# Attention in two halves over two steps, in a fused state-space and attention kernel

## The chip, the core and the metric

The kernel runs on one core of a Trainium2 chip. The core has four compute engines that work side by side, each through its own list of instructions in order: TensorE (PE, matrix products and transposes, with a separate track PEld for loading weights), VectorE (DVE), ScalarE (ACT) and GpSimd (POOL). SyncE (SP) issues the transfers (DMA). Operands lie in SBUF; matrix products land in PSUM. The metric is the time of one whole execution on the device, in microseconds (us), lower is better.

## The reference

The input x is 16 images of 128 channels and 64 x 64 positions, so 16 sequences of 4096 tokens of 128 numbers. A first layer adds a selective state-space block; a second adds an attention with one fixed query per head and then a mixture of 64 experts. Cut to what the change touches:

```python
# layer 0, after GroupNorm: a recurrence over the tokens, d = 256 channels, n = 16 states
xc    = silu(causal_conv4(xs) + conv_b)
dt, Bm, Cm = split(xc @ W_xproj)
delta = softplus(dt @ W_dt + b_dt)
h_t   = exp(delta_t * A) * h_{t-1} + (delta_t * xc_t) * B_t      # per channel and state
y_t   = sum_n h_t * C_t
out   = (y + xc * D_param) * silu(z) @ W_out                      # added to x, transposed in height and width

# layer 1, after LayerNorm: 8 heads, a running softmax over all tokens up to t
k, v  = silu(x @ W_kv)                       # per head 128 numbers each
s     = q_proj . k
m_A   = cummax(s)
u_A   = cumsum(exp(s - m_A))
w_A   = cumsum(exp(s - m_A) * v)
output = mean over heads of w_A / u_A        # added to x
# then: LayerNorm, top-8 tokens for each of 64 experts, two-layer experts, scattered back
```

## The kernel before

The sequences are cut into blocks of 512 tokens: 8 blocks each, 128 in all. A main loop makes one *step* per block k. A step has 16 *slots*, one for each state n. In it four blocks are in work: block k in the recurrence; block k + 1 in the convolution, x-projection and delta; block k - 1 in its output projection; and block m = k - 9 in the attention. A wrapper keeps each engine's instructions in the order of the text; before the change the transfers, issued through `nc.sync`, are not under it.

The recurrence, with one scan per state and half of the channels:

```python
dap = tile_pool("dap", bufs=8); hp_ = tile_pool("hp", bufs=2); bcp = tile_pool("bcp", bufs=4)   # abridged
ps  = tile_pool("ps", bufs=3, space=PSUM); acc = tile_pool("acc", bufs=1, space=PSUM)           # abridged

def load_bc(k, n):        # B and C of one state, spread to 128 rows
    t = w["bc", n] = bcp.tile([P, 2, L], F32, tag="bc", name="bct")
    nc.sync.dma_start(t, w["bcs"][n : n + N + 1 : N, :].partition_broadcast(P))

def decay(k, n):
    for a in range(NH2):
        ACT.activation(da[:, a, :], w["delta"][:, a, :], AF.Exp, scale=a_neg[:, a, n : n + 1])

def scan(k, n):
    bx = bps.tile([P, NH2, L], F32, tag="bx", name="bx")                    # PSUM
    DVE.tensor_tensor(bx, w["du"], bc(bt[:, 0:1, :], [P, NH2, L]), ALU.mult)   # the product with B
    for a in range(NH2):
        DVE.tensor_tensor_scan(h[:, a, :], da[:, a, :], bx[:, a, :], <0.0 or state>, ALU.mult, ALU.add)
    POOL.tensor_tensor(da, h, bc(bt[:, 1:2, :], [P, NH2, L]), ALU.mult)     # the product with C

def keep_state(k, n):     # the last column, for the next block
    ACT.copy(gn[w["b"]]["state"][:, n, :], h[:, :, L - 1])

def add_y(k, n):          # eight transposes that add up in PSUM
    ...
```

The attention of a block of 512 tokens, in four chunks c of 128. A weight from token t' to token t is exp((s - m) at t' minus log u at t), computed as a product of two small matrices plus a mask:

```python
lh = wp.tile([P, L], F32, name="lh")            # 5 rows in each half in use
rh = wp.tile([P, L // P, 4, P], F32, name="rh")

def score_max(m):   # VectorE: running maximum, then s - max -> le; four transfers le -> lh
def score_exp(m):   # ScalarE: e = exp(le)
def score_sum(m):
    DVE.tensor_tensor_scan(s["mx"], bc(ones[:, 0:1], [P, L]), s["e"], ..., ALU.mult, ALU.add)
    ...             # TensorE: e transposed; ScalarE: to e1
def score_log(m):   # ScalarE: log; eight transfers mx -> rh; ScalarE: e = exp(-log)

def weights(m, c):
    for u in range(2):
        rows = slice(64 * u, 64 * u + 5)
        PE.matmul(rp, identb, bc(maskb.unsqueeze(1), [P, 4, P]), start=True, stop=False)
        PE.matmul(rp, lh[rows, bass.ts(c, P)], rh[rows, c].rearrange("p x t -> p (x t)"), start=False, stop=True)
        ACT.activation(wm[:, u].rearrange("p q g t -> p (q g t)"), rp, AF.Exp)

def attend(m, c):         # eight products weights x values -> ao_ps, eight narrow ones -> carry_ps
def carry_on(m, c):       # VectorE: carry += carry_ps
def attend_before(m, c):  # TensorE: what earlier chunks carry to this one
def finish(m):            # VectorE: xt += ao_ps / 8; transfer to t2_d
```

One step, cut to the parts that move:

```python
def slot(n):
    if n == 0:  attend(mp_, 3); attend_before(mp_, 2); add_y(prev, 14); key(m, 0..2); carry_on(mp_, 2)
    if n == 1:  attend_before(mp_, 3); add_y(prev, 15); key(m, 3..4); carry_on(mp_, 3); finish(mp_); score(m, 0); ...
    if n == 3:  load_exp(); score(m, 1); score_max(m); gate(prev)
    if n == 4:  out_proj(prev); score_exp(m); conv(nxt, 0)
    if n == 5:  residual(prev); score_sum(m); conv(nxt, 1)
    if n == 6:  score_log(m)
    if n == 7:  conv_silu(nxt); gate_silu(cur); xproj(nxt)
    if 7 <= n <= 9: value(m, ...)
    if n == 9:  delta(nxt)
    if n == 10: load_exp(); ln_center(mn)      # and its square on ScalarE
    if n == 11: ln_scale(mn)
    if 11 <= n <= 14: weights(m, n - 11)
    if n >= 12: attend(m, 0), (m, 1), (m, 2) in slots 12, 13, 14; carry_on(m, 0) in 13, carry_on(m, 1) in 15
    if n == 13: ln_apply(mn)

for n in range(N):
    scan(cur, n); load_bc(n + 4); keep_state(cur, n - 1)
    if n == N - 1: delta_x(nxt)
    slot(n)
    add_y(cur, n - 2)
    if 3 <= n <= 6 or n >= 10: decays(k, n, 2)     # up to five states ahead
    if n == 12: gn_stats(...)                      # GroupNorm of a coming sequence
    if n == 14 and <last block>: gn_end(...)       # once in eight steps
```

Behind the main loop stand three stages that the change leaves as they are: the routing of tokens to experts, the experts, and the scatter back.

Of the kernel before, what the change touches and what calls it, by code (L numbers as in the profile page):

```python
# [39 lines left out]
def conv_attn_hybrid(ctx: ExitStack, tc: tile.TileContext, x, w_in, conv_w, conv_b, w_xproj, w_dt, b_dt,  # L40
# [72 lines left out]
    with ExitStack() as st:  # L113
# [5 lines left out]
        PE, DVE, ACT, POOL = (InOrder(tc, e) for e in (nc.tensor, nc.vector, nc.scalar, nc.gpsimd))  # L119
# [32 lines left out]
        lh = wp.tile([P, L], F32, name="lh")  # L152
        rh = wp.tile([P, L // P, 4, P], F32, name="rh")
# [6 lines left out]
        nc.vector.memset(lh, -1.0)  # L160
        for x in range(4):
            nc.vector.tensor_copy(rh[:, :, x, :], bc(ident[:, x : x + 1].unsqueeze(2), [P, L // P, P]))
        for x in range(4):
            nc.vector.tensor_copy(rh[64:, :, x, :], bc(ident[64:, 64 + x : 65 + x].unsqueeze(2), [64, L // P, P]))
# [40 lines left out]
        xsp = st.enter_context(tc.tile_pool(name="xsp", bufs=1))  # L205
        mp = st.enter_context(tc.tile_pool(name="mp", bufs=2))
        m1 = st.enter_context(tc.tile_pool(name="m1", bufs=1))
        dap = st.enter_context(tc.tile_pool(name="dap", bufs=8))
# [24 lines left out]
        def gn_load(b, i):  # L233

            if i == 0:
                gn[b] = dict(stats=stp.tile([P, NBLK, 6], F32, tag="stats", name="stats"))
            t = xsp.tile([P, L], F32, tag="xs", name="xs")
            nc.sync.dma_start(t, x_f[b, :, bass.ts(i, L)])
            gn[b]["t"] = t
# [22 lines left out]
        def load_block(k):  # L262

            b, i = divmod(k, NBLK)
            t = xbp.tile([P, KC - 1 + L], F32, tag="xb", name="xb")
            if i == 0:
                POOL.memset(t[:, : KC - 1], 0.0)
                nc.sync.dma_start(t[:, KC - 1 :], x_f[b, :, :L])
            else:
                nc.sync.dma_start(t, x_f[b, :, i * L - (KC - 1) : (i + 1) * L])  # L270
            blocks[k] = dict(k=k, b=b, i=i, xb=t)
# [28 lines left out]
        def xproj(k):  # L300


            w = blocks[k]
            pt = bank("dbl_ps")
            for a in range(NH2):
                PE.matmul(pt[:NX, :], wx[:, a, :], w["xc"][:, a, :], start=(a == 0), stop=(a == NH2 - 1))
            dbl = w["dbl"] = m1.tile([NX, L], F32, tag="dbl", name="dbl")
            ACT.copy(dbl, pt[:NX, :])
            bcs = w["bcs"] = bcd.tile([2 * N, L], F32, tag="bcs", name="bcs")
            nc.sync.dma_start(bcs, dbl[R:, :])  # L310
# [21 lines left out]
        def load_bc(k, n):  # L332
            w = blocks[k]
            t = w["bc", n] = bcp.tile([P, 2, L], F32, tag="bc", name="bct")
            nc.sync.dma_start(t, w["bcs"][n : n + N + 1 : N, :].partition_broadcast(P))
# [6 lines left out]

        def scan(k, n):
# [5 lines left out]
            bt, da = w.pop(("bc", n)), w["da", n]  # L349
            bx = bps.tile([P, NH2, L], F32, tag="bx", name="bx")  # L350
            DVE.tensor_tensor(bx, w["du"], bc(bt[:, 0:1, :], [P, NH2, L]), ALU.mult)
# [52 lines left out]
        def load_residual(b):  # L404
            res[b] = xp.tile([P, T], F32, tag="xt", name="xt")
            nc.sync.dma_start(res[b], x_f[b])
# [13 lines left out]
        def ln_center(m):  # L420
            b, i, xs = where(m)
            s = att[m] = dict(cen=bank("cen_ps"))
            PE.matmul(s["cen"], cmat, xs, start=True, stop=True)
            s["sq"] = short("sq")
            ACT.activation(s["sq"], s["cen"], AF.Square)
# [9 lines left out]
        def ln_apply(m):  # L435
            s = att[m]
            s["xn"] = a1.tile([P, L], F32, tag="xn", name="xn", bufs=2)
            DVE.tensor_tensor(s["xn"], s.pop("cen"), s.pop("rstd"), ALU.mult)
# [17 lines left out]
        def score_max(m):  # L456
# [5 lines left out]
            s["le"] = a1.tile([P, L], F32, tag="le", name="le")  # L462
# [3 lines left out]
            DVE.tensor_tensor(s["le"], s["s"], mx, ALU.subtract)  # L466

            for u in range(2):
                for q in range(2):
                    r = 64 * u + 32 * q  # L470
                    nc.sync.dma_start(lh[64 * u + 2 * q : 64 * u + 2 * q + 2, :], s["le"][r : r + 2, :])

        def score_exp(m):
            s = att[m]
            s["e"] = a1.tile([P, L], F32, tag="e", name="e")
            ACT.activation(s["e"], s.pop("le"), AF.Exp)

        def score_sum(m):
# [4 lines left out]
            DVE.tensor_copy(gn[b]["den"], s["mx"][:, L - 1 : L])  # L483
            et = bank("et_ps")
# [5 lines left out]
        def score_log(m):  # L490
            s = att[m]
            ACT.activation(s["mx"], s["mx"], AF.Ln)
            for u in range(2):
                for q in range(2):
                    r = 64 * u + 32 * q
                    for g in range(2):
                        nc.sync.dma_start(rh[64 * u + 4 : 64 * u + 5, :, 2 * q + g, :], s["mx"][r + g : r + g + 1, :])
# [13 lines left out]
        def weights(m, c):  # L511
# [3 lines left out]
            for u in range(2):  # L515
                rows = slice(64 * u, 64 * u + 5)
                rp = bank("w_ps")
                PE.matmul(rp, identb, bc(maskb.unsqueeze(1), [P, 4, P]), start=True, stop=False)
                PE.matmul(rp, lh[rows, bass.ts(c, P)], rh[rows, c].rearrange("p x t -> p (x t)"),
# [3 lines left out]
        def attend(m, c):  # L523
# [3 lines left out]
            if c == 0:  # L527
                s["o"] = acc.tile([P, L], F32, tag="acc", name="ao_ps")
            cols, v, wm = bass.ts(c, P), s.pop(("v", c)), s.pop(("wm", c))
            for h in range(HD):  # L530
                g, j = divmod(h, 4)

                PE.matmul(s["o"][:, cols], v[:, h, :], wm[:, j // 2, j % 2, g, :], start=(c == 0 and h == 0),
# [16 lines left out]
        def attend_before(m, c):  # L550
            s = att[m]
            if m % NBLK or c:
                PE.matmul(s["o"][:, bass.ts(c, P)], carry[:, (c - 1) % 4, :], s["e"][:, bass.ts(c, P)], start=False,
                          stop=True, skip_group_check=True)

        def finish(m):
            b, i, xs = where(m)
            s = att.pop(m)
            DVE.scalar_tensor_tensor(xs, s["o"], 1.0 / HD, xs, ALU.mult, ALU.add)
            nc.sync.dma_start(t2_d[b, :, bass.ts(i, L)], xs)  # L560
# [6 lines left out]
        LEAD = 5  # L567
# [28 lines left out]
        for n in range(4):  # L596
            load_bc(0, n)
        decays(0, 0, 5)

        for k in range(NK + LAG + 1):  # L600
# [10 lines left out]
            def slot(n):  # L611

                if n == 0:
                    if mp_ is not None:
                        attend(mp_, 3)
                        attend_before(mp_, 2)
# [4 lines left out]
                    if mp_ is not None:  # L621
                        carry_on(mp_, 2)
                if n == 1:
                    if mp_ is not None:
                        attend_before(mp_, 3)
# [4 lines left out]
                    if mp_ is not None:  # L630
                        carry_on(mp_, 3)
                        finish(mp_)
                    if m is not None:
# [14 lines left out]
                if n == 3:  # L648
                    load_exp()
# [3 lines left out]
                    if prev is not None:  # L653
                        gate(prev)
                if n == 4:
                    if prev is not None:
                        out_proj(prev)
                    if m is not None:
                        score_exp(m)
                    if nxt is not None:  # L660
                        conv(nxt, 0)
                if n == 5:
                    if prev is not None:
                        residual(prev)
                    if m is not None:
                        score_sum(m)
                    if nxt is not None:
                        conv(nxt, 1)
                if n == 6 and m is not None:
                    score_log(m)  # L670
                if n == 7:
                    if nxt is not None:
                        conv_silu(nxt)
                    if cur is not None:
                        gate_silu(cur)
                    if nxt is not None:
                        xproj(nxt)
                if 7 <= n <= 9 and m is not None:
                    for x in ((0, 1), (2, 3, 4), (5, 6, 7))[n - 7]:
                        value(m, x // 2, x % 2)  # L680
                if n == 9 and nxt is not None:
                    delta(nxt)
                if n == 10:
                    load_exp()
                    if mn is not None:
                        ln_center(mn)
                if n == 11 and mn is not None:
                    ln_scale(mn)
                if m is not None:
                    if 11 <= n <= 14:  # L690
                        weights(m, n - 11)
                    if n >= 12:
                        c = n - 12
                        if c < 3:
                            attend(m, c)
                        if c == 1:
                            attend_before(m, 0)
                            carry_on(m, 0)
                        if c == 3:
                            attend_before(m, 1)  # L700
                            carry_on(m, 1)
                if n == 13 and mn is not None:
                    ln_apply(mn)

            for n in range(N):
                if cur is not None:
                    scan(cur, n)
                    later = k * N + n + 4
                    if later < NK * N and order[later][0] in blocks and "bcs" in blocks[order[later][0]]:
                        load_bc(*order[later])  # L710
                    if n:
                        keep_state(cur, n - 1)
                    if n == N - 1 and nxt is not None:
                        delta_x(nxt)
                if prev is not None and n == 0:
                    keep_state(prev, N - 1)
                slot(n)
                if cur is not None and n >= 2:
                    add_y(cur, n - 2)
                if 3 <= n <= 6 or n >= 10:  # L720
                    decays(k, n, 2)
# [3 lines left out]
                if n == 0 and i == 1 and cur is not None:  # L725
# [3 lines left out]
                if n == 12 and stat is not None:  # L729
                    gn_stats(*stat)  # L730
# [161 lines left out]
```

## Time and profile before

| What | Value |
|---|---|
| time, median of 3 | 13180.21 us (13174.85 to 13191.18) |
| PE busy | 11484.8 us, 87% of the span |
| DVE busy | 9947.5 us, 75% |
| ACT busy | 7080.3 us, 54% |
| POOL busy | 6336.2 us, 48% |
| mean granted TensorE clock | 0.886 |
| DMA queue of the transfers | 1390.92 MB, 40.8% of 16 engines |

The profile is one execution on the chip as the hardware's profiler took it. Busy shares are averages over stages with different limits, so the span is also given in 40 slices and in chosen stretches. A busy TensorE isn't a TensorE at its peak: its clock may be granted in full (1.00) or in half (0.50). Nearly all instructions of the main loop carry the line number of the wrapper (L31), so groups are told apart by the names of their tiles, output first: `bx<-du,bct` is the product with B, `h<-da,state,bx` the scan, `da<-h,bct` GpSimd's product with C, `y_ps<-ident,da` the transposes that add up y, `w_ps<-rh,lh` the log weights, `ao_ps<-wm,v` weights times values. "Idle before" is the time an engine stood still ahead of an instruction, and the arrow names what released it.

### The profile page before, as it was taken

The numbers are of one execution on the slowest core, as the hardware profiler recorded it, in microseconds if no ns is written. First come the engines' busy times: TensorE is split into PE (matmuls) and PEld (weight loads), VectorE is DVE, ScalarE is ACT, GpSimd is POOL, SyncE is SP. The second block draws the span as 40 slices with busy tenths as digits, with TensorE's granted clock in tenths as the row PEclk, the third lists the DMA queues.
The fourth block names the chain that finished last, engine by engine and source line by source line (L and its number), as shares of the span: only waits on it lengthen the run. The fifth ranks groups of instructions, "written<-read, shape, count | busy, mean of one in ns | idle before, by whom it ended". The sixth has DMA issues, their size and how long they took to land. (4 is left out here: it accounts for less than half of the span.)

```text
span 13178.4 us, 153074 instructions
## 1 busy us (share of the span) xinstructions
PE 11484.8 (87%) x55359; PEld 6609.2 (50%) x55359; DVE 9947.5 (75%) x8977; ACT 7080.3 (54%) x12594; POOL 6336.2 (48%) x2590
## 2 busy tenths in 40 slices
PE   5588989889888989898989889888988898988887
PEld 3344555555455545554555555545555555444464
DVE  7988888888888888888888888888888888124422
ACT  4456555656565655566555656565656565432210
POOL 5655555555555555555555555555555555012310
PEclk7689999999999999999989999999999999888975
DMA  4544444444444444444444444444444443011127
GB/s 129 125 112 106 111 106 114 109 107 109 110 108 111 107 106 113 106 113 106 112 103 113 109 109 107 112 109 107 110 105 113 102 112 96 7 48 45 52 81 290
DMA packets 693703, 1400.71 MB, mean 106 GB/s; under 512 B 51072, under 2 KB 89616, under 8 KB 684752
## 3 DMA queue, kind: packets, MB, share of 16 engines
q1 hardware_dynamic: 692944, 1390.92, 40.8%
q8 instruction: 436, 7.14, 0.2%
q14 instruction: 323, 2.65, 0.1%
HBM read 1294.25 MB, written 92.27 MB: 105 GB/s over the span
## 5 line engine op out<-in xcount | busy, mean ns | idle before, releaser
L31 POOL TENSOR_TENSOR da<-h,bct 128x1024 f32<-128x1024 f32 x2048 | 6034.0, 2946 | 5154.1 <-DVE h L31 1812.6
L31 DVE TENSOR_TENSOR_SCAN h<-da,state,bx 128x512 f32<-128x512 f32 x3584 | 4392.4, 1267 | 578.3 <-ACT state L31 389.5
L31 DVE TENSOR_TENSOR bx<-du,bct 128x1024 f32<-128x1024 f32 x2048 | 3090.6, 1509 | 43.8 <-DMA bct<-bcs 2.9
L31 ACT ACTIVATE da<-delta,a_neg 128x512 f32<-128x512 f32 x4096 | 2639.6, 711 | 365.2 <-PE y_ps L31 359.1
L31 PE MATMUL y_ps<-ident,da 128*128 128x128 f32 x16384 | 2280.9, 287 | 154.5 <-POOL da L31 153.5
L31 PEld LDWEIGHTS y_ps<-ident,da 128*128 128x128 f32 x16384 | 1957.4, 148 | 900.4 <-issue 635.3
L31 ACT ACTIVATE wm<-w_ps 128x512 f32<-128x512 f32 x1024 | 608.7, 594 | 1561.7 <-PE w_ps L31 1559.1
L31 PEld LDWEIGHTS ao_ps<-wm,v 128*128 128x128 f32 x8192 | 1268.4, 244 | 346.5 <-issue 346.5
L31 PE MATMUL ao_ps<-wm,v 128*128 128x128 f32 x8192 | 1369.3, 336 | 0.0
L31 PE MATMUL w_ps<-rh,lh 5*128 5x512 f32 x2048 | 1320.7, 728 | 0.0
L31 PE MATMUL xs_ps<-xb,wc 128*128 128x512 f32 x2048 | 987.5, 627 | 304.1 <-DVE xt L31 302.3
L31 PE MATMUL k_ps<-xn,wk 128*128 128x512 f32 x2048 | 988.4, 615 | 55.2 <-DVE carry L31 55.2
L31 ACT ACTIVATE kt<-k_ps 128x512 f32<-128x512 f32 x1024 | 586.9, 602 | 755.3 <-PE k_ps L31 755.3
L31 PE MATMUL v_ps<-wv,xn 128*128 128x512 f32 x2048 | 964.9, 605 | 6.6 <-ACT z L31 3.3
L31 ACT ACTIVATE v<-v_ps 128x512 f32<-128x512 f32 x1024 | 610.4, 598 | 477.1 <-PE v_ps L31 477.1
L107 POOL TENSOR_SCALAR diag<-ident,rstd 128x128 f32<-128x128 f32 x512 | 299.1, 602 | 1164.5 <-DVE rstd L96 1100.1
L31 PEld LDWEIGHTS xs_ps<-xb,wc 128*128 128x128 f32 x2048 | 402.0, 202 | 797.6 <-issue 438.8
L31 DVE TENSOR_TENSOR_SCAN h<-da,bx 128x512 f32<-128x512 f32 x512 | 597.0, 1208 | 88.4 <-ACT state L31 60.1
L31 DVE TENSOR_TENSOR carry<-carry,carry_ps 128x128 f32<-128x128 f32 x496 | 135.9, 274 | 693.0 <-PE carry_ps L31 693.0
L31 PEld LDWEIGHTS k_ps<-xn,wk 128*128 128x128 f32 x2048 | 367.8, 196 | 483.3 <-issue 451.5
L31 ACT COPY state<-h 128x2 f32<-128x2 f32 x1792 | 334.2, 187 | 487.0 <-DVE h L31 486.5
L31 PEld LDWEIGHTS v_ps<-wv,xn 128*128 128x128 f32 x2048 | 363.3, 192 | 453.2 <-issue 430.8
(163 smaller groups left out, 11528.7 us busy)
## 6 DMA issues: line engine op xcount, KB each, us to landing
bct<-bcs SPq DMA_DIRECT2D x2048, 512.0 KB
xs<-in_x_dram SPq DMA_DIRECT2D x128, 256.0 KB
xt<-in_x_dram SPq DMA_DIRECT2D x16, 2048.0 KB
t_d<-xt SPq DMA_DIRECT2D x128, 256.0 KB
t<-t_d SPq DMA_DIRECT2D x64, 512.0 KB
tc<-t_d SPq DMA_DIRECT2D x16, 2048.0 KB
out_dram<-tc SPq DMA_DIRECT2D x16, 2048.0 KB
xb<-in_x_dram SPq DMA_DIRECT2D x112, 257.5 KB
```

The source lines that it names most:

```text
L31: return lambda *args, **kw: self.tc.keep_in_program_order(f(*args, **kw))
L107: nc.gpsimd.tensor_scalar(diag[:, c, :], ident, rstd[:, k : k + 1], None, ALU.mult)
```

## The change

It has four parts.

1. **The attention in two halves over two steps.** Chunks 0 and 1 of a block are attended at the end of its own step (slots 12 to 15), chunks 2 and 3 in slots 3 to 7 of the next. Each half has its own accumulator and its own `finish`. The running sum, its logarithm and the transposition of the weights move to later slots. The aim is to spread TensorE's work over the step.
2. **VectorE's other work behind the product with B.** The product with B is split from the scan and stands first in a slot; carries, gate, residual and the like follow it and precede the scan. The aim is that the product doesn't meet GpSimd's product with C, and that the small work lies beside that one.
3. **Log weights by products of all 128 rows.** `lh` becomes two tiles with zeros in the unused rows, so that one product reads 128 rows and not 5. The number of transfers of log sums falls from eight to four.
4. **The DMA queue in order of the text.** SyncE goes under the wrapper; B and C are loaded two states ahead of use and not four.

With them go: decays up to six states ahead in nine buffers, the statistics' input in a shared pool, and the residual's load in slot 7 with its output product set aside once in eight steps.

```diff
-        PE, DVE, ACT, POOL = (InOrder(tc, e) for e in (nc.tensor, nc.vector, nc.scalar, nc.gpsimd))
+        PE, DVE, ACT, POOL, SP = (InOrder(tc, e) for e in (nc.tensor, nc.vector, nc.scalar, nc.gpsimd, nc.sync))
...
-        lh = wp.tile([P, L], F32, name="lh")
-        rh = wp.tile([P, L // P, 4, P], F32, name="rh")
+        lh = [wp.tile([P, L], F32, name=f"lh{u}") for u in range(2)]
+        rh = wp.tile([P, 4, L], F32, name="rh")
...
-        dap = st.enter_context(tc.tile_pool(name="dap", bufs=8))
+        dap = st.enter_context(tc.tile_pool(name="dap", bufs=9))
...
+        def product(k, n):
+            w = blocks[k]
+            bx = w["bx"] = bps.tile([P, NH2, L], F32, tag="bx", name="bx")
+            DVE.tensor_tensor(bx, w["du"], bc(w["bc", n][:, 0:1, :], [P, NH2, L]), ALU.mult)
...
+        def set_aside(k):
+            w = blocks[k]
+            o = short("o")
+            ACT.copy(o, w["o"])
+            w["o"] = o
...
-                    for g in range(2):
-                        nc.sync.dma_start(rh[64 * u + 4 : 64 * u + 5, :, 2 * q + g, :], s["mx"][r + g : r + g + 1, :])
+                    SP.dma_start(rh[64 * u + 4 : 64 * u + 5, 2 * q : 2 * q + 2, :], s["mx"][r : r + 2, :])
...
-                PE.matmul(rp, lh[rows, bass.ts(c, P)], rh[rows, c].rearrange("p x t -> p (x t)"),
+                PE.matmul(rp, lh[u][:, bass.ts(c, P)], rh[:, :, bass.ts(c, P)],
                           start=False, stop=True)
...
-            if c == 0:
+            if c % 2 == 0:
                 s["o"] = acc.tile([P, L], F32, tag="acc", name="ao_ps")
...
-        def finish(m):
+        def finish(m, half):
...
-        LEAD = 5
+        LEAD = 6
```

The new step, with the same cuts as above:

```python
def before(n):
    if n == 7:  score_sum(m)
def beside(n):
    if n == 0:  add_y(prev, 14); key(m, 0..2); finish(mp_, 0)
    if n == 1:  add_y(prev, 15); key(m, 3..4); score(m, 0); ...
    if n == 3:  score(m, 1); score_max(m); gate(prev); weights(mp_, 2)
    if n == 4:  weights(mp_, 3); attend(mp_, 2)
    if n == 5:  spread_weights(m); out_proj(prev); attend(mp_, 3); attend_before(mp_, 2)
    if n == 6:  score_exp(m); carry_on(mp_, 2); conv(nxt, 0); residual(prev)      # or set_aside(prev)
    if n == 7:  attend_before(mp_, 3); conv(nxt, 1); carry_on(mp_, 3); finish(mp_, 1); conv_silu(nxt)
    if n == 8:  gate_silu(cur); turn_weights(m); xproj(nxt)
    if 8 <= n <= 10: value(m, ...)
    if n == 11: delta(nxt); ln_center(mn); load_exp(); score_log(m)
    if n == 12: ln_square(mn); ln_scale(mn); weights(m, 0)
    if n == 13: weights(m, 1); attend(m, 0); attend_before(m, 0)
    if n == 14: ln_apply(mn); attend(m, 1); carry_on(m, 0)
    if n == 15: attend_before(m, 1); carry_on(m, 1)

for n in range(N):
    before(n)
    if n == 0: delta_x(k)
    product(cur, n)
    if n == 12: gn_stats(...)
    if n == 3: load_exp()
    if 3 <= n <= 7: decays(k, n, 2)                # up to six states ahead
    beside(n)
    if n >= 11: decays(k, n, 2)
    load_bc(n + 2)
    scan(cur, n); keep_state(cur, n - 1)
    add_y(cur, n - 2)
    if n == 14 and <last block>: gn_end(...)
```

## The prediction

> **What bounds the kernel now.** I began with the page's busy shares in 40 slices, because the kernel has stages with different limits.
>
> ```profile
> PE   5588989889888989898989889888988898988887
> DVE  7988888888888888888888888888888888124422
> PEclk7689999999999999999989999999999999888975
> ```
>
> Slices 3 to 34 are one long stage (the recurrence with the attention). TensorE and VectorE both stand at 0.8 to 0.9 there and neither is full, so the step is set by waits between two nearly equal engines. Next I took busy time by stretch: ten thousand us of that stage, then one whole step, from its first key product to that of the next step, then two short pieces of it (columns: stretch, length, busy time and instruction count of PE, PEld, DVE, ACT, POOL, granted clock, DMA share, GB/s).
>
> ```profile
> 1000.00:11000.00 10000.00, 8970.31 (x44481) 5087.69 (x44480) 8338.49 (x7346) 5964.46 (x10707) 5339.03 (x1832) 0.92 0.44 109
> ...
> 6006.59:6091.94 85.35, 76.89 (x395) 43.95 (x393) 74.05 (x65) 52.61 (x96) 47.09 (x16) 0.94 0.46 109
> ...
> 6066.00:6069.00 3.00, 3.00 (x14) 1.56 (x13) 2.87 (x2) 2.95 (x7) 1.32 (x1) 0.97 0.87 214
> 6069.00:6072.00 3.00, 3.00 (x26) 2.36 (x26) 2.21 (x4) 2.05 (x5) 0.75 (x1) 0.50 0.57 150
> ```
>
> In the third row TensorE computes log weights; in the fourth, straight after, its clock is half. A clock of 0.92 costs TensorE 8% of each step, about 7 us. Third, VectorE's timeline beside GpSimd's, in order of time (start, length).
>
> ```profile
> 6042.62 1.23 DVE L31 TENSOR_TENSOR bx<-du,bct 128x1024 f32<-128x1024 f32 x1
> 6043.98 2.45 DVE L31 TENSOR_TENSOR_SCAN h<-da,state,bx 128x512 f32<-128x512 f32 x2
> ...
> 6064.63 0.67 DVE L31 BATCH_NORM_STATS2 stats<-xs 128x6 f32<-128x512 f32 x1
> 6065.21 3.20 DVE L31 TENSOR_TENSOR bx<-du,bct 128x1024 f32<-128x1024 f32 x1
> ```
>
> ```profile
> 6042.84 3.21 POOL L31 TENSOR_TENSOR da<-h,bct 128x1024 f32<-128x1024 f32 x1 [0.64 <-PE z_ps L31]
> ...
> 6064.97 2.36 POOL L31 TENSOR_TENSOR da<-h,bct 128x1024 f32<-128x1024 f32 x1 [1.22 <-ACT wm L31]
> ```
>
> When the product with B starts straight behind a scan it takes 1.23 us, and GpSimd's product stretches to 3.21. When a small VectorE operation comes between, GpSimd starts first (2.36 us) and the product with B takes 3.20. Last, VectorE's and TensorE's waits over the same ten thousand us (total, times, longest).
>
> ```profile
> DVE h L31 <- ACT state L31: 427.4, 459, 2.7
> DVE carry L31 <- PE carry_ps L31: 380.6, 112, 7.2
> DVE xt L31 <- PE ao_ps L31: 236.4, 113, 3.3
> DVE mx L31 <- PE s_ps L31: 229.2, 114, 2.2
> DVE gs L31 <- PE gn_ps L31: 142.0, 14, 10.9
> ```
>
> ```profile
> PE xs_ps L31 <- DVE xt L31: 293.6, 114, 3.0
> PE z_ps L31 <- ACT xc L31: 246.3, 114, 2.7
> PE o_ps L31 <- DVE z L31: 203.1, 114, 1.8
> ```
>
> Each engine waits for the other in turn: VectorE where TensorE is crowded (attention, end of the step), TensorE where VectorE is (slots 3 to 7). "Slot" is one n of the 16 states of a step.
>
> **What the Trainium skill says.** "SBUF — State Buffer", section "SBUF: two separate sides": VectorE and GpSimd share a port pair as an exclusive lock; a VectorE operation with two SBUF inputs and a GpSimd operation that reads SBUF block each other for a whole instruction, whoever starts first wins. The 1.23/3.21 and 3.20/2.36 pairs above agree. "TensorE: Matmul & The Clock Gate", section "Part 1: The HAM clock gate", says that TensorE runs at half clock after a window of low activity (it gives about 3.4 us for a window). The 0.50 above agrees in size; but TensorE was busy throughout the stretch before it, so here "low activity" has to be products that use 5 of 128 rows. The page does not say that row count matters; the trace only puts the two side by side.
>
> **The change, part by part.** Log weights: 8 products per step with 128 rows in place of 5. One pair takes 1.37 us now (bfloat16 mask 0.31, float32 part 1.06, start to start in the timeline); a full-row float32 product of that width goes at 0.86 (three keys in 2.58). If 128 rows go like a key, 8 x 0.20 = 1.6 us less. More is in the clock: perhaps two thirds of the 7 us of capacity, on the path only where TensorE sets the pace.
>
> Product with B: mean 1509 ns on the page against 1232 undisturbed, so 16 x 0.28 = 4.4 us a step. I expect one loss to stay: the running sum of weights (2529 ns mean now) reads SBUF twice and stands before the product in slot 7, so GpSimd may come between (2 us).
>
> The move of half of the attention evens TensorE. I summed each engine's work by groups of four slots from the instruction order of the kernel before and after. TensorE: transposes of y 0.87 a slot, key or value 0.86, a score half 0.99, convolution 3.44, output product 1.82, gate product 1.72, x-projection 1.7, delta 1.9, an attention chunk 1.88 + 0.57, a weights chunk 2.74 before and 2.34 after. Before: 17.2, 17.9, 14.9, 19.7 us. After: 16.5, 19.9, 17.0, 14.5. VectorE has 3.85 a slot (product start to product start) plus its other work: before, with 4.4 of port waits spread evenly, 21.0, 20.4, 16.5, 19.6; after, with the one port wait in slot 7, 20.3, 21.0, 15.4, 17.3. (What it has besides: scores and gate 3.3 in slot 3, residual 1.25, running sum 1.4 without the port wait, delta times x 1.2, statistics 0.67, normalized tokens 0.69, four carries of 0.27, the attention's end 0.69 or two of 0.42.) Buffers tie the engines within about a slot of one another (a scan waits for the state copy two slots back, a transpose of y for GpSimd two slots back), so I take the larger of the two in each group: before 21.0 + 20.4 + 16.5 + 19.7 = 77.6, after 20.3 + 21.0 + 17.0 + 17.3 = 75.6.
>
> The step measured before is 85.35, so 7.7 us lie in the half clock, hand-offs and crowding inside groups. For after I keep about 5.4: less clock, but a new chain on ScalarE in slots 11 to 13. There, delta (1.3), a table load (1.3), log and exponential (1.3) and two decays (2.5) now stand ahead of the square that the variance product waits for. With TensorE's last free work done, that is some 4 us of TensorE idle, and the scan of slot 13 behind it waits for its state copy. So 75.6 + 5.4 = 81 us.
>
> The GroupNorm end comes once in 8 steps. VectorE waits up to 10.9 us there because TensorE is late at the step's end (14 waits, 142.0 us: 1.3 a step). After the change TensorE is early there, so I keep 0.5: 81.5 a step.
>
> Sum. The product delta times x starts from 72.3 to 11108.1 us, 128 times; the intervals without attention are 72.7 each (212.5 to 721.6 in 7). So (11035.8 - 9 x 72.7) / 118 = 88.0 us per attention step. Gain 119 x (88.0 - 81.5) = 774. First 9 steps: the gate, residual, statistics and delta-times-x no longer (or less) let GpSimd in, 5.5 each, 50. The last ten steps, attention alone (480 us at clock 0.86): 25. The routing, experts and output stages behind are untouched. 13180 - 850 = 12330 us.
>
> **Rivals.** One: evening works better than I think and VectorE alone is the bound. Its floor after is 74.0 a step with the one port wait; at 76 the gain is 119 x 12 = 1430, time 11,700. For it: nothing on VectorE but the scores then waits directly for TensorE. Against: before, 77.6 by the same sum became 85.35.
>
> Two: ScalarE's chain in slots 11 to 13 and a PSUM bank shortage (two carry banks and the output bank are all held in slots 5 and 6, so the convolution waits for VectorE) eat most of it: 85 a step, about 12,750. For it: the 246.3 and 293.6 us of exactly such waits now.
>
> Three: the transfers. Loads of B and C lead by two slots instead of four and stand in the queue behind the log weights, the block store and the 2048 KB residual. DMA is busy 0.44 and VectorE waited for B and C twice in the whole run (2.9 us), so I expect up to 2 us a step; if the queue stalls in each step for 4 us or more, the time is near 12,900. Four: the clock does not rise, since the many transposes and narrow carry products remain; that costs about 2 us a step, 12,550.
>
> **Range and chances.** The middle, 81.5, lies between 77.5 (gain 1325) and 85 (gain 430): 11,900 to 12,720. Faster than 12,917 (2%) needs a step under about 86; I give 0.85. The same 0.10, for the queue or a bank shortage; slower 0.05, for a wait that I have not seen.
>
> **What would show it right or wrong.** The product with B near 1.25 us mean, GpSimd's near 3.1; the clock in the stage at 0.95 or more; the 128-row product near 0.6 us per record in place of 0.692; the GroupNorm wait of VectorE under 60 us in all; TensorE waiting for the square in slot 12; a new wait of VectorE on B and C of some tens to 200 us. The step would prove wrong if VectorE's waits on TensorE and on state copies did not fall, or if waits on DMA passed 300 us.

## The result

| | Time, median | Ratio to before |
|---|---|---|
| before | 13182.35 us (13174.85 to 13191.18) | 1 |
| changed | 12850.71 us (12841.71 to 12861.79) | 0.9749, 95% interval 0.9732 to 0.9765 |

The change wins 332 us, where 850 were forecast; 12,851 lies above the range of 11,900 to 12,720. By the prediction's own division (starts of delta times x from 43.8 to 10845.2 us, the first nine intervals together 622.8 in the trace) an attention step takes (10801.4 - 622.8) / 118 = 86.3 us. It was 88.0 and was forecast at 81.5.

The page of the changed kernel, busy share and granted clock in 40 slices:

```profile
PE   5688888888888888888888888888888888988887
DVE  8988888888888888888888888888888888134422
PEclk7799999999999999999999999999999999998865
```

TensorE's row is flatter and in places a tenth lower; VectorE's looks no fuller (of ten thousand us it is busy 8,568, and was 8,338). So neither engine took up the room: there are waits, and they are not the old ones. VectorE's, TensorE's and ScalarE's longest over the same ten thousand us as before:

```profile
DVE h L31 <- ACT state L31: 440.4, 231, 3.9
DVE bx L31 <- DMA bct<-bcs: 393.7, 281, 2.8
DVE mx L31 <- PE s_ps L31: 334.7, 116, 11.4
DVE carry L31 <- PE carry_ps L31: 27.9, 19, 7.7
...
DVE gs L31 <- PE gn_ps L31: 6.6, 14, 0.5
```

```profile
PE yb_ps L31 <- ACT kt L31: 606.2, 114, 6.7
PE var_ps L31 <- ACT sq L31: 515.8, 117, 4.5
```

```profile
ACT xb L31 <- DMA xb<-in_x_dram: 550.4, 114, 6.2
```

In the kernel before, TensorE's two were short, and ScalarE's wait for x isn't in the list at all:

```profile
PE var_ps L31 <- ACT sq L31: 65.7, 114, 0.6
...
PE yb_ps L31 <- ACT kt L31: 43.3, 114, 0.4
```

VectorE's waits at the crowded end of the step did go: carries from 380.6 to 27.9, GroupNorm from 142.0 to 6.6, the end of the attention from 236.4 to 0.3. In their place stand two waits on transfers (B and C, and the block of x), and a wait for the scores that has grown. One step shows how these hang together. First SyncE's queue, then ScalarE, TensorE, VectorE and GpSimd, all from one step:

```profile
6021.11 0.33 SPq L31 DMA_DIRECT2D t_d<-xt  x1
6021.54 0.38 SPq L31 DMA_DIRECT2D bct<-bcs  x1
6022.01 0.44 SPq L31 DMA_DIRECT2D xb<-in_x_dram  x1
```

```profile
6027.87 0.81 ACT L31 ACTIVATE xb<-xb,gs 128x512 f32<-128x512 f32 x1 [4.71 <-DMA xb<-in_x_dram]
...
6030.76 1.57 ACT L31 ACTIVATE kt<-k_ps 128x512 f32<-128x512 f32 x3
```

```profile
6031.41 1.97 PE L31 MATMUL yb_ps<-ident,yt 128*128 128x128 f32 x8 [5.12 <-ACT kt L31]
```

```profile
6016.26 1.20 DVE L31 TENSOR_TENSOR du<-delta,xc 128x1024 f32<-128x1024 f32 x1
6017.49 3.26 DVE L31 TENSOR_TENSOR bx<-du,bct 128x1024 f32<-128x1024 f32 x1
6020.67 0.41 DVE L31 SCALAR_TENSOR_TENSOR xt<-ao_ps,xt 128x256 f32<-128x256 f32 x1
...
6038.14 1.28 DVE L31 TENSOR_TENSOR_SCAN mx<-negc,mx,s_ps 128x512 f32<-128x512 f32 x1 [5.76 <-PE s_ps L31]
...
6056.36 1.25 DVE L31 TENSOR_TENSOR_SCAN mx<-ones,den,e 128x512 f32<-128x512 f32 x1
...
6057.71 3.14 DVE L31 TENSOR_TENSOR bx<-du,bct 128x1024 f32<-128x1024 f32 x1
```

```profile
6016.60 3.06 POOL L31 TENSOR_TENSOR da<-h,bct 128x1024 f32<-128x1024 f32 x1 [5.84 <-DVE h L31]
...
6056.66 3.10 POOL L31 TENSOR_TENSOR da<-h,bct 128x1024 f32<-128x1024 f32 x1 [1.76 <-DVE h L31]
```

The block store of the attention's first half waits for VectorE's `finish` in slot 0 (the line at 6020.67). The next block of x stands two places behind it, with a load of B and C between; it is issued at 6022.0 and needed by ScalarE in slot 1. ScalarE can start on it at 6027.9, after standing for 4.7 us. Behind that in ScalarE's list are the last three keys; TensorE waits 5.1 us for them and then runs its eight transposes in 1.97 us instead of 1.14 in the step of before, since the granted clock from 6031 to 6036 us is 0.50; VectorE waits 5.8 us for the scores. One late transfer is seen as three waits, and only the first of them names it. In the step of before, SyncE issued the next block at 6050.39, in the middle of the step ahead of the one that needs it.

### The profile page after: what moved, and what is told of

Same layout as the page of the kernel before. It is cut to its first block, busy times and chain, and to the rows that moved or that the text cites. A ratio compares the mean times of both kernels' runs of the same rounds, so it can differ in the third digit from the quotient of the medians.

```text
span 12840.0 us, 152607 instructions
## 1 busy us (share of the span) xinstructions
PE 10745.1 (84%) x55359; PEld 6573.2 (51%) x55359; DVE 10032.5 (78%) x9111; ACT 7105.8 (55%) x12611; POOL 6597.7 (51%) x2590
## 5 line engine op out<-in xcount | busy, mean ns | idle before, releaser
L31 POOL TENSOR_TENSOR da<-h,bct 128x1024 f32<-128x1024 f32 x2048 | 6295.5, 3074 | 4621.6 <-DVE h L31 3415.9
L31 DVE TENSOR_TENSOR bx<-du,bct 128x1024 f32<-128x1024 f32 x2048 | 3292.5, 1608 | 469.7 <-DMA bct<-bcs 412.1
L31 PE MATMUL w_ps<-rh,lh 128*128 128x512 f32 x2048 | 1148.4, 644 | 11.9 <-DMA rh<-mx 11.7
L31 PEld LDWEIGHTS ao_ps<-wm,v 128*128 128x128 f32 x8192 | 984.4, 192 | 181.3 <-issue 177.7
L31 PE MATMUL ao_ps<-wm,v 128*128 128x128 f32 x8192 | 998.5, 275 | 0.0
L31 PE MATMUL xs_ps<-xb,wc 128*128 128x512 f32 x2048 | 936.3, 600 | 7.6 <-issue 1.8
L31 PE MATMUL yb_ps<-ident,yt 128*128 128x128 f32 x1024 | 243.3, 416 | 644.6 <-ACT kt L31 622.7
L31 PE MATMUL var_ps<-sq,mean_w 128*128 128x512 f32 x256 | 242.7, 1047 | 552.6 <-ACT sq L31 552.6
L31 PEld LDWEIGHTS w_ps<-rh,lh 128*128 128x128 f32 x2048 | 439.6, 215 | 441.6 <-issue 391.2
L31 PEld LDWEIGHTS xs_ps<-xb,wc 128*128 128x128 f32 x2048 | 370.0, 191 | 403.3 <-issue 373.1
```

The source lines that it names most:

```text
L31: return lambda *args, **kw: self.tc.keep_in_program_order(f(*args, **kw))
```

## The experiments

The kernel before, run beside them, took 13,182 to 13,184 us. "Changed" is the changed kernel, 12,851. Each edit is to the kernel named in its heading.

### e1: the changed kernel, the block of x one step sooner

```diff
-                if n == 0 and nxt is not None:
-                    load_block(nxt)
+                if n == 9 and k + 2 < NK:
+                    load_block(k + 2)
```

> The changed kernel, with the next block of x loaded one step sooner (slot 9 of the step before, instead of slot 0 of the same step). Theory A (the late load): the load of x stands in the queue behind the block store and a load of B and C, ScalarE waits 550 us for it in 9,500 us, the last three keys wait behind ScalarE, TensorE then waits 606 us for the keys and VectorE 335 us for the scores; so the step falls by 4 to 5 us, time 12,250 to 12,400, and all three waits drop under 150 us. Theory B (ScalarE's chain in slots 11 to 13 sets the pace, and slack won early in a step is lost there): the waits for x vanish, but the time stays above 12,700. Theory C (VectorE's waits for B and C): as B, above 12,700, with waits for B and C grown.

12,349 us (ratio 0.9366, 0.9352 to 0.938): 502 us less than changed. The waits for x and for the scores are off the list, and TensorE's for the keys, 558.4 us in 9,000 in the changed kernel, is down to:

```profile
PE yb_ps L31 <- ACT kt L31: 41.9, 109, 0.4
```

That is theory A. The time is also the one that the prediction gave for the whole change; how far that was luck is said below.

### e2: the changed kernel, the square ahead of the decays of slot 11

```diff
+                    if mn is not None:
+                        ln_square(mn)         # slot 11, behind score_log
...
-                        ln_square(mn)         # slot 12
```

> The changed kernel, with ScalarE's square of the centred tokens ahead of the decays of slot 11 instead of behind them. Theory A (the late load of x): TensorE's wait for the square (516 us) halves, the time falls by under 120 us, to 12,730 or more. Theory B (ScalarE's chain in slots 11 to 13): 2.5 us less a step and a full clock behind it, 12,450 to 12,550.

12,692 us (0.9628, 0.9612 to 0.9644): 159 less, more than A allowed and far less than B. TensorE's wait for the square fell from 463 to 204 us in 9,000. ScalarE's chain costs something, but isn't the bound.

### e3: the changed kernel, B and C ahead of the slot's other transfers

```diff
                     product(cur, n)
+                    later = k * N + n + 2
+                    if later < NK * N:
+                        load_bc(*order[later])
                 ...
-                    later = k * N + n + 2     # behind beside(n)
-                    if later < NK * N:
-                        load_bc(*order[later])
                     scan(cur, n)
```

> The changed kernel, with the load of B and C put in the queue ahead of the other transfers of its slot. Theory A: the load of x gets later still by nothing, and only the 394 us of waits for B and C shrink, so 100 to 200 us less, about 12,700. Theory C (waits for B and C in slots 10 and 13 are on the path in full, 3.4 us a step): 300 to 400 us less, 12,450 to 12,550.

12,341 us (0.9364, 0.935 to 0.9377): 510 less, more than either theory. VectorE's and ScalarE's waits on transfers, in 9,000 us (360.7 and 507.0 in the changed kernel):

```profile
DVE bx L31 <- DMA bct<-bcs: 19.6, 27, 1.4
```

```profile
ACT xb L31 <- DMA xb<-in_x_dram: 166.6, 106, 3.1
```

I had overlooked that the load of B and C in slot 0 no longer waits for the half-block store, so it no longer stands between that store and the block of x. The store still does stand straight ahead of x, and yet two thirds of the wait for x are gone: in one step x is issued at 5994.18, directly behind the store, and ScalarE starts on it 3.0 us later, where it took 5.9 us in the step above. So the lateness came from the store and the load of B and C behind it together. One edit removed most of two waits; VectorE's wait for state copies rose from 402 to 713 us.

### e4: the changed kernel, the queue out of the order of the text

```diff
-        PE, DVE, ACT, POOL, SP = (InOrder(tc, e) for e in (..., nc.sync))
+        PE, DVE, ACT, POOL = (InOrder(tc, e) for e in (...))
+        SP = nc.sync
```

> The changed kernel, with the transfers no longer held to the order of the text (one part of the change undone). Theory A: the load of x goes back to well ahead of its use, as before the change, where it led by about 50 us; the wait of ScalarE for x vanishes and the time falls to 12,300 to 12,500. Theory B or C: within 100 us of the changed kernel, or slower because loads of B and C come later.

12,663 us (0.9607, 0.9592 to 0.9621): only 188 less, which is short of A's range and more than B or C allowed. The wait for x did vanish, as A says. But now TensorE waits for the log sums (156 us, up to 9.8) and for B and C (92, up to 10.2) ahead of the log weights, and VectorE 948 us for state copies (402 in the changed kernel). Giving up the order altogether is no full cure; e3 and e9 narrow down which place in it is at fault.

### e5: the kernel before, 128-row log weights alone

```diff
-        lh = wp.tile([P, L], F32, name="lh")
+        lh = [wp.tile([P, L], F32, name=f"lh{u}") for u in range(2)]      # zeros in unused rows
...
-                PE.matmul(rp, lh[rows, bass.ts(c, P)], rh[rows, c].rearrange("p x t -> p (x t)"),
+                PE.matmul(rp, lh[u][:, bass.ts(c, P)], rh[:, c].rearrange("p x t -> p (x t)"),
```

> The kernel before, with one part of the change alone: log weights by products of all 128 rows. Theory A (few rows count as little activity, so they halve the clock): the clock of the attention stage rises from 0.92 to 0.95 or more, the weights-times-values products fall from 336 ns mean to under 300, and 200 to 450 us are won. Theory B (the half clock comes from TensorE's idle gaps and transposes, not from the row count): the clock stays within 0.01, and only the shorter product counts, 8 x 0.2 us a step, at most 190 us won.

12,630 us (0.958, 0.9564 to 0.9596): 552 us, more than theory A's upper end and more than the whole change. The stage's row has a clock of 0.97, and weights times values, whose own code is the same, runs at 276 ns, not 336:

```profile
1000.00:10000.00 9000.00, 7739.34 (x41968) 4615.07 (x41967) 8033.39 (x6930) 5599.93 (x10087) 5026.90 (x1726) 0.97 0.44 114
```

```profile
L31 PE MATMUL ao_ps<-wm,v 128*128 128x128 f32 x8192 | 1005.5, 276 | 0.0
```

The product itself is shorter too. In full clock a pair of mask and log weights took 1.37 us from start to start; here one starts at 6084.53 and the next at 6085.61, 1.08 us. Eight pairs save 2.3 us a step, at most some 270 us in 118 steps (an estimate), so theory B doesn't reach 552 us even with the measured product.

VectorE's waits for TensorE fell as well, though the attention stands where it stood. In 9,000 us those for the attention's end, GroupNorm and the carries were 214.2, 132.1 and 333.1 before; now they are:

```profile
DVE xt L31 <- PE ao_ps L31: 137.9, 102, 1.4
DVE gs L31 <- PE gn_ps L31: 61.3, 14, 4.4
...
DVE carry L31 <- PE carry_ps L31: 0.3, 1, 0.3
```

### e6: e1, back to 5-row log weights

```diff
-                PE.matmul(rp, lh[u][:, bass.ts(c, P)], rh[:, :, bass.ts(c, P)],
+                rows = slice(64 * u, 64 * u + 5)
+                PE.matmul(rp, lh[u][rows, bass.ts(c, P)], rh[rows, :, bass.ts(c, P)],
```

> The changed kernel with the block of x loaded one step sooner, and the log weights back to products of 5 rows. Theory A (row count and clock): the clock of the stage falls from 0.95 to 0.93 or less and the time rises by 120 to 350 us above the 12,349 of the same kernel with 128 rows. Theory B (gaps and transposes): the clock stays, the time rises by less than 120, since TensorE has slack now.

13,489 us (1.0234, 1.0216 to 1.0252): 1,140 us more than e1, over three times theory A's upper end, and slower than the kernel before. The clock is 0.85:

```profile
1000.00:10000.00 9000.00, 8331.63 (x38854) 4648.61 (x38854) 7181.20 (x6519) 5251.81 (x9347) 4823.07 (x1600) 0.85 0.40 106
```

```profile
L31 PE MATMUL ao_ps<-wm,v 128*128 128x128 f32 x8192 | 1417.6, 345 | 0.0
```

With the attention in two halves, 5-row products stand at two places of a step, and the clock falls at both: in one step they run from 6054 to 6065 us and from 6110 to 6121, and the clock is 0.50 from 6060 to 6069 and from 6108 to 6124 (the second stretch begins just ahead of its products). Without the 128 rows the rest of the change, with x on time, would have lost 306 us to the kernel before.

### e7: e1, the product with B last

```diff
-                    product(cur, n)           # first in the slot
...
                 if cur is not None:
+                    product(cur, n)           # straight ahead of the scan
                     ...
                     scan(cur, n)
```

> The changed kernel with the block of x loaded one step sooner, and the product with B moved behind VectorE's other work of the slot, straight ahead of the scan, as it was before the change. Theory A (the shared port): GpSimd then starts first in slots 0, 3, 6, 7, 12, 14 and 15, the product there takes 2 to 3.3 us, and the longer of GpSimd's 2.36 and the small work is paid each time, some 6 us a step less what lies under other waits of slots 12 to 15: 250 to 700 us above 12,349. Theory B (the order is hidden under waits for ScalarE and for B and C): within 100 us of 12,349.

12,552 us (0.9521, 0.9507 to 0.9536): 203 more than e1, between the theories. The product's mean rises to 1782 ns from e1's 1567, so the port order works as the Trainium skill has it ("SBUF — State Buffer", section "SBUF: two separate sides": who starts first keeps the port for the whole instruction); much of the 6 us a step is won back elsewhere, as A had allowed for in part: in 9,000 us VectorE's waits for B and C fall from 371 to 74 us and those for state copies from 331 to 211.

### e8: the three moves of e1, e2 and e3 together

> The changed kernel with three moves at once: the block of x one step sooner, the square ahead of the decays, B and C ahead of the other transfers of their slot. If the first and third cure the same wait (the late block of x), their gains of 502 and 510 us hardly add, and with the square's 159 the time is 12,050 to 12,250. If they cure different waits, the gains add to some 1,170: under 11,800.

12,029 us (0.9124, 0.911 to 0.9137): 822 less than changed, where the three alone sum to 1,171. The moves of e1 and e3 do overlap: if e1's 502 and e2's 159 count in full, 161 are left for the third. No run has two of the moves alone, so how the 822 divide isn't shown.

### e9: e5, plus the queue in order of the text

```diff
-            nc.sync.dma_start(...)            # all transfers of the main loop
+            SP.dma_start(...)
-                    later = k * N + n + 4
+                    later = k * N + n + 2
```

> The kernel before with 128-row log weights (12,630), plus the queue in order of the text with B and C two states ahead (the residual's load put behind slot 1, where the order lets it be). Theory A1 (the order alone makes the block of x late): ScalarE waits for x some 4 us a step and the time rises by 200 us or more. Theory A2 (the block is late only together with the half-block store that the split puts ahead of it in slot 0): ScalarE's wait for x stays under 100 us in all, the time within 100 us of 12,630.

12,677 us (0.9616, 0.9601 to 0.963): 47 more than e5, and ScalarE doesn't wait for x at all in 9,000 us: theory A2. The order by itself costs little (VectorE waits 127 us for B and C). The some 500 of e1 come when the split also puts the half-block store, and behind it a load of B and C, ahead of x in slot 0.

### e10: e5, plus the product with B first, no split

```diff
-                    scan(cur, n)              # product and scan together, ahead of the slot
+                    product(cur, n)
+                slot(n)
+                if cur is not None:
+                    scan(cur, n)
```

> The kernel before with 128-row log weights (12,630), plus the product with B ahead of VectorE's other work, the attention not split. Theory A (the port order is worth what moving it back cost, 203 us): 12,400 to 12,480, and the split is then worth little beside it. Theory B (the order helps only once the split has evened TensorE, since without it VectorE stands waiting for TensorE between product and scan): 12,550 or more.

12,358 us (0.9372, 0.9356 to 0.9388): 272 less than e5, theory A. The edit puts the whole slot ahead of the scan, so the order of the other engines' work moves with VectorE's, and the 272 are the sum of both. The product with B and its idle time, on e10's page:

```profile
L31 DVE TENSOR_TENSOR bx<-du,bct 128x1024 f32<-128x1024 f32 x2048 | 3018.3, 1474 | 69.6 <-DMA bct<-bcs 3.7
```

Two of the four parts, with no split and no ordered queue, are as fast as e1 with all four and its block of x on time (12,349).

### e11: e8, one decay in slots 11 and 12

```diff
-                    decays(k, n, 2)
+                    decays(k, n, 1 if n < 13 else 2)
```

> The kernel with the three moves (12,029), plus one decay and not two on ScalarE in each of slots 11 and 12, the rest later. Theory (ScalarE's chain there still sets the pace of slots 12 to 14, which take 6.7, 5.8 and 5.6 us in place of 4.5, 3.9 and 4.8): scans wait less for state copies (471 us now) and the time falls by 150 to 350. Rival (VectorE itself is the bound by now): under 80.

11,977 us (0.9086, 0.9072 to 0.9099): 52 less, the rival's size. VectorE still waits 454 us for state copies, so the theory falls; the rival isn't shown either, since VectorE is busy 8,230 of 9,000 us and not all of them. What holds the copies there stays open. It is the fastest of all these kernels.

## Why the prediction was wrong

**The failed step** is the third rival. It asked what the queue's new order would do to B and C, said "up to 2 us a step", and named nothing else in the queue. B and C measured 393.7 us in ten thousand, some 116 steps, so 3.4 a step: under-sized. The block of x wasn't in the sum at all, neither among the rivals nor in the 5.4 us a step kept for waits: e1 shows 502 us, 4.3 for each of 118 steps, which is the distance between 81.5 forecast and 86.3 measured but for 0.5. It could have been read from the text: the load stands behind a store that waits for VectorE in slot 0 and behind a load of B and C, and its reader stands in slot 1. Two of the prediction's own signs of being wrong came true: waits on DMA passed 300 us (550.4 for x, 393.7 for B and C), and VectorE's waits for state copies did not fall (427.4 before, 440.4 after).

**The sum for the rest** came out right by luck (e1: 12,349 against 12,330). By the same division e1's step is 81.9 us for 81.5 forecast, but the terms behind it were mis-sized and made up for one another:

- *Log weights.* 1.6 us of work and a part of 7 us of clock. e5 shows 552 us alone. The mechanism, few rows and then a half clock, is what e5 and e6 show: only the rows change, and the clock goes from 0.92 to 0.97 and from 0.95 to 0.85. How the chip counts few rows isn't shown, only that the clock moves with them. The size was too small: in full clock the product saves 2.3 us and not 1.6, and the rest of the 552 goes with the clock. The duration was about right: a median of 592 ns a record in the changed kernel and in e5, for 0.6 us forecast and 692 before (the means, 644, 592 and 728, hold stretches of half clock as well). The fourth rival's transposes and narrow products leave at most 0.03 of clock in e5. The changed kernel has 0.94: in the step above half clock follows TensorE's new idle time, and e8, with most of that idle time gone, has 0.97.
- *Product with B.* A mean near 1.25 us was forecast; it is 1608 ns. Slot 7 loses its 2 us as foreseen (3.14). Slot 0 loses the same (3.26), since delta times x also reads SBUF twice and GpSimd gets in between it and the product: GpSimd's product ends 2.2 us behind delta times x, and the product with B 1.1 us after that. I had counted that slot as cured. Where B and C come late, GpSimd may have started by then; e8, where VectorE hardly waits for them, has a mean of 1494 ns. The gain of the order is 272 us in e10 and 203 in e7, some 2 us a step, close to 4.4 less the 2 of one slot.
- *The split.* I took the larger engine of each group of four slots and gave the evening part of the step's gain. Much of the evening isn't the split's: in e5 the waits for carries are already gone, and GroupNorm's halved, with the attention where it was. What the split adds is the attention's end (137.9 us in 9,000 in e5, 0.3 in the changed kernel's ten thousand) and the rest of GroupNorm's. And e10 without the split is as fast as e1 with it (12,358 and 12,349). In e1 there are waits that e10 lacks: TensorE's for the square (491 us in 9,000, 63 in e10) and VectorE's for B and C (371; 3.7 in all of e10). Where both are cut, in e8, the split kernel takes 12,029, 329 less than e10. These kernels also differ in the queue's order and the lead of the decays, so what the split is worth by itself is not shown.

**Right were** ScalarE's chain in slots 11 to 13 ("some 4 us of TensorE idle": 515.8 us over 116 steps is 4.4; e2, which cuts it by more than half, gains only 159 us), GpSimd's product (3074 ns, for 3.1 us), the end of the GroupNorm wait (6.6 us, under 60 forecast), and the new wait on B and C, though at twice the size. The clock, 0.94, just missed the 0.95 or more.

The sums have small slips that change nothing here: the gain counts 119 steps where the division has 118 (7 us); 4 us a step for the queue come to about 12,810 and not 12,900; a step of 85 us comes to 12,750 and not 12,720. And the 7 us of clock are reckoned from 0.92, where the step in hand had 0.94, which makes 5.

## What to carry to other kernels

When a queue is put in order of the text, go through every transfer in it: what the one ahead waits for, and how many slots lie before its reader. A small store that waits for an engine delays all that stand behind it, a load between takes its own time on top, and the wait then shows under other names two engines on. Before work is moved to even two engines, try the parts that change no order: here a matrix filled up with zeros, alone, won more (552 us) than the whole change that it was part of (332).

## What the runs showed that I had not expected

Filling 5 rows up to 128 with zeros made a product shorter (a pair with its mask from 1.37 to 1.08 us in full clock) and raised the granted clock for everything near it: from 0.92 to 0.97 in one kernel, from 0.85 to 0.95 in another, worth 552 and 1,140 us. Two VectorE operations that both read SBUF twice, issued one behind the other or with a copy of 0.15 us between, don't keep GpSimd out: it has its turn between them, and the second takes 3.26 and 3.14 us for 1.23.
